# Mixture-of-experts layer of a graph network: experts as 191 register-addressed units of 196 rows instead of 64 fixed blocks of 784, 12 more tiles of edge counts beside them, and the source tiles of the clears and fills moved into the scatter stage's memory

## The chip, the cores and the metric

One Trainium2 chip, one core. The metric is the device time of one execution in microseconds (us), lower is better. The engines are PE (TensorE, matrix products), DVE (VectorE), ACT (ScalarE), POOL (GpSimd) and SP (SyncE, which here only issues DMA transfers and loads its registers). Each engine runs its own list of instructions in order and waits on semaphores. DMA transfers are issued from SP's list, from ACT's (both plain copies) and from POOL's (indirect gathers and scatters of rows).

## The reference

Four graph layers on 12,500 nodes of 128 features with 200,000 edges (`src` random, `dst` sorted and skewed towards low numbers). After each layer `x = layernorm(x + layer(x))`.

- Layer 0: points on a hyperbolic ball, a weighted sum over each node's edges, and the way back.
- Layer 1: a normalised sum over the edges times `W_conv` (`new_feats`), then a mixture of experts, then batch normalisation over the nodes of the sum of both.
- Layers 2 and 3: two more edge sums, the last followed by a small network and a residual.

The experts are what the change touches:

```
scores = x @ gate_W + gate_b                    # 12,500 x 64
topv, topi = top_k(scores, 2)                   # each node goes to two experts
pos = rank of the pair (node, expert) within its expert;  valid = pos < 782
buf[expert, pos] = x                            # 64 x 782 x 128, zero where no pair is
y = gelu(buf @ W1 + b1) @ W2 + b2               # W1 128x256, W2 256x128 per expert
out = sum over the two experts of softmax(topv) * y[expert, pos]
```

25,000 pairs go into 64 experts of at most 782 rows, so about half of the rows of `buf` are blank.

## The kernel before, in words

The nodes are 98 tiles of 128 (`NT`, `P`). The stages follow each other, and the end of each is marked by what the next reads; times are those of the profiled execution.

**Preparation (0 to about 200 us).** `points` (lines 446 to 487) maps the nodes to the ball and writes 14 groups of rows (`table<-parts`); columns of the edge list are loaded and turned (lines 531 to 630). On SP's list among these stand clears of `msg` (`clear`, line 523, the source is the tile `blank`, 396 KB each, 99 in all and three smaller ones for the last tile) and fills of `buf` with zeros (line 670, the source is the tile `zero`, 448 KB each, 56 in all). `msg` is a DRAM array in which every edge will have a row, and a row without an edge must hold zeros; `buf` holds the experts' rows. Tile, the framework that the kernel is written in, puts the instructions of most stages into an order of its own, so SP's list doesn't follow the text: 51 of the clears and 8 of the fills are issued in this stage.

**Scatter (213 to 2734 us).** `spread_edges` (lines 489 to 770) runs 391 iterations of 512 edges. In each, `fetch` (lines 654 to 670) broadcasts the edges' row numbers (`rb`), loads a number from `first_r` into an SP register (line 657), and loads the window of table rows at that address (`win`, line 661); every so often it also issues a clear or, in every sixth iteration, a fill. PE picks the edges' rows by one-hot products (lines 695 and 701), DVE multiplies them by the weights (line 722), ACT casts them into one of six `rows` buffers (line 734), and POOL scatters them into `msg` (line 751). The order of DVE, PE and ACT is written out by hand here (`manual_schedule`); SP's and POOL's is the scheduler's.

**Collecting, first edge sums, routing (2740 to 5124 us).** Collecting reads `msg` back in large transfers. The routing (lines 1314 to 1393) forms `new_feats` and the gate scores, takes the top two, and counts per expert in the tile `run` (each partition its part of the pairs per expert), from which each pair's row `expert * SL + pos` follows. POOL scatters 196 times 128 rows into `buf` (line 1388), the last one starting at 5122.1 us. `SL` is 784 rows per expert, seven tiles of `TT` = 112.

**Experts (5124 to 5716 us, lines 1398 to 1442).** For each of 64 experts: SP loads `w1` and `w2` (lines 1411, 1413; 128 KB each), ACT's list loads a broadcast bias `b2` and the 784 rows `xt` (lines 1415, 1417), PE transposes seven tiles (line 1422), DVE copies them into `bT` (lines 1423, 1424), four products of 392 columns (line 1429) go to PSUM, ACT does the gelu (line 1431), fourteen products (line 1436) give `pw` again, DVE adds the bias (line 1439) and SP stores 784 rows to `ybuf` (line 1440). All addresses are fixed.

Beside the experts stand the **band counts** (`band_counts`, line 1252) of the later edge sums: for a node tile, DVE makes one-hot marks (`fs` line 1073, `fd` line 1075), PE multiplies them in about 17 matmuls (`fb_ps`, line 1089), ACT casts four banks (line 1091) and SP stores 512 KB (line 1093). `EXB` = 48 of the 98 tiles are written in the experts' loop, the other 50 in the combining loop; the scheduler interleaves them with their neighbours, and starts some before the first expert.

**Combining (5716 to 6045 us, lines 1470 to 1480).** For each node tile POOL gathers 128 rows of `ybuf` twice (`yk`, line 1476), DVE multiplies by the gates and adds (line 1479), `stats` accumulates the sums of the batch normalisation (line 1451). Then the normalisation and the two last edge sums, up to 8278 us.

Of the kernel before, what the change touches and what calls it, by code (L numbers as in the profile page):

```python
# [40 lines left out]
TT = 112  # L41
NTT = 7
SL = TT * NTT
# [24 lines left out]
EXB = 48  # L68
# [70 lines left out]
def gnn_kernel(ctx: ExitStack, tc: tile.TileContext, a, out: bass.AP):  # L139
# [65 lines left out]
    ybuf = dram.tile([DUMP, D], F32, name="ybuf")  # L205
# [283 lines left out]
    def spread_edges(bad):  # L489
# [5 lines left out]
        with tc.tile_pool(name="sc", bufs=1) as pc, tc.tile_pool(name="scp", bufs=1, space=PSUM) as pps:  # L495
# [19 lines left out]

            blank = pc.tile([P, RB - SURE, W3], BF16, name="blank")
            V.memset(blank, 0.0)
            V.memset(blank[:, :, 3 * W0:3 * W0 + 1], -1.0)
            V.memset(blank[:, :, 3 * W0 + 1:3 * W0 + 3], 127.0)

            def clear(t, b0, b1):
                r0 = t * RS
                return Y.dma_start(msg[r0 + b0 * P:r0 + b1 * P, :].rearrange("(b p) f -> p b f", p=P),
                                   blank[:, 0:b1 - b0, :])

            if True:
# [105 lines left out]
                px_.close()  # L632
                for b in range(SURE_LAST, RB, RB - SURE):
                    clear(NT - 1, b, min(b + RB - SURE, RB))

            with tc.tile_pool(name="sb", bufs=4) as lp, tc.tile_pool(name="sw", bufs=3) as wk, \
                    tc.tile_pool(name="sg", bufs=2, space=PSUM) as gp:
                step = 7 * D
                zero = pc.tile([P, step], F32, name="zero")
                V.memset(zero, 0.0)  # L640
                bz = buf[0:DUMP, :].rearrange("(p r) f -> p (r f)", p=P)
                empty = list(range(NT - 1))
                fill = list(range(0, DUMP // P * D, step))
# [10 lines left out]
                def fetch(i):  # L654
# [13 lines left out]
                    if i % 6 == 5 and fill:  # L668
                        r = fill.pop(0)
                        Y.dma_start(bz[:, r:r + step], zero)  # L670
# [631 lines left out]
    with tc.tile_pool(name="moe", bufs=1) as pm:  # L1302
# [95 lines left out]
        with tc.tile_pool(name="ex", bufs=2) as wk, tc.tile_pool(name="exb", bufs=2, space=PSUM) as pb, \  # L1398
                tc.tile_pool(name="exh", bufs=2, space=PSUM) as ph_, tc.tile_pool(name="exc", bufs=1) as pc, \
                band_pools("x") as band:  # L1400
            b1n = pc.tile([NE, HID], F32, name="b1n")
            Y.dma_start(b1n, a["L1_gnn_b1"])
            b1T = pc.tile([P, 2, NE], F32, name="b1T")
            for j in range(2):
                pb1 = ph_.tile([P, 512], F32, name="ph")
                T.transpose(pb1[:, 0:NE], b1n[:, j * P:(j + 1) * P], ident[:NE, :NE])
                V.tensor_copy(b1T[:, j, :], pb1[:, 0:NE])
            HALF = SL // 2
            for e in range(NE):
                w1 = wk.tile([P, HID], F32, name="w1")  # L1410
                Y.dma_start(w1, a["L1_gnn_W1"][e])
                w2 = wk.tile([P, 2, D], F32, name="w2")
                Y.dma_start(w2, a["L1_gnn_W2"][e].rearrange("(j p) d -> p j d", p=P))
                b2 = wk.tile([TT, D], F32, name="b2")
                S.dma_start(b2, a["L1_gnn_b2"][e].partition_broadcast(TT))
                xt = wk.tile([TT, NTT, D], F32, name="xt")
                S.dma_start(xt, buf[e * SL:(e + 1) * SL, :].rearrange("(i p) f -> p i f", p=TT))
                px = pb.tile([P, 1024], F32, name="pw")
                bT = wk.tile([P, SL], F32, name="bT")
                for i in range(NTT):  # L1420
                    o = i * TT if i < 4 else 512 + (i - 4) * TT
                    T.transpose(px[:, o:o + TT], xt[:, i, :], ident[:TT, :TT])
                V.tensor_copy(bT[:, 0:4 * TT], px[:, 0:4 * TT])
                V.tensor_copy(bT[:, 4 * TT:SL], px[:, 512:512 + 3 * TT])
                hT = wk.tile([P, 2, SL], F32, name="hT")
                for j in range(2):
                    for q in range(2):
                        ph = ph_.tile([P, 512], F32, name="ph")
                        T.matmul(ph[:, 0:HALF], w1[:, j * P:(j + 1) * P], bT[:, q * HALF:(q + 1) * HALF],
                                 start=True, stop=True)  # L1430
                        S.activation(hT[:, j, q * HALF:(q + 1) * HALF], ph[:, 0:HALF], AF.Gelu,
                                     bias=b1T[:, j, e:e + 1])
                py = pb.tile([P, 8, D], F32, name="pw")
                for i in range(NTT):
                    for j in range(2):
                        T.matmul(py[:TT, i, :], hT[:, j, i * TT:(i + 1) * TT], w2[:, j, :],
                                 start=(j == 0), stop=(j == 1))
                ye = wk.tile([TT, NTT, D], F32, name="ye")
                V.tensor_tensor(ye, py[:TT, 0:NTT, :], b2[:, None, :].to_broadcast([TT, NTT, D]), OP.add)
                Y.dma_start(ybuf[e * SL:(e + 1) * SL, :].rearrange("(i p) f -> p i f", p=TT), ye)  # L1440
                for s in range(EXB * e // NE, EXB * (e + 1) // NE):
                    band_counts(band, s)
# [168 lines left out]
```

## Time and profile before

| | us |
|---|---|
| median of six executions | 8261.73 |
| lowest, highest | 8241.03, 8314.44 |
| the profiled execution: its time | 8280.44 |
| the profiled execution: its span in the trace | 8278.6 |
| preparation | 0 to about 200 |
| scatter | 213 to 2734 |
| experts, from the first weight load to the end | 5124.5 to 5716 |
| combining | 5716 to 6045 |

PE is busy 63% of the span, DVE 52%, POOL 47%, ACT 24%; the mean granted clock of PE is 0.919. Shares over the whole span say little here, because each stage has its own limit; they are read stage by stage.

How to read the lines: a group's line has the line of the kernel, the engine, the operation, `out<-in` by the program's names, the shapes where asked for, a count, then busy time in us, mean duration of one in ns, and the engine's idle time just before these instructions with what ended it. An engine's name with q (SPq, ACTq) is its list of issued transfers and register operations; their durations are given as minimum/median/maximum in ns.

### The profile page before, as it was taken

How to read it: one execution, taken by the hardware profiler on the slowest of the kernel's cores; microseconds unless marked ns; L12 is line 12 of the kernel's file. 1: busy time of each engine (PE TensorE's matmuls, PEld its weight loads, DVE VectorE, ACT ScalarE, POOL GpSimd, SP SyncE). 2: the span in 40 equal slices, each digit the busy share in tenths (PEclk: the TensorE clock that was granted, in tenths of full speed). 3: DMA queues.
4: the chain of work that ended last, by engine and by line, in shares of the span. 5: the costliest groups of instructions: out<-in, count | busy, mean ns of one | idle time of the engine just before them, and what ended most of it. 6: DMA issues, size and time to landing. Idle time of an engine off the chain costs nothing. (4 is left out here: it accounts for less than half of the span.)

```text
span 8278.6 us, 106434 instructions
## 1 busy us (share of the span) xinstructions
PE 5230.9 (63%) x32620; PEld 3153.9 (38%) x33009; DVE 4299.5 (52%) x11730; ACT 1976.7 (24%) x4176; POOL 3863.5 (47%) x3917
## 2 busy tenths in 40 slices
PE   0444444444444556388878644998717988588995
PEld 0333333333333223144444423765303444234444
DVE  6666666666666678655555355555881123301115
ACT  3222222232222122222222111443440001100003
POOL 0555555566666100366665454002716665466650
PEclk9999999999999988699999856998958999799998
DMA  9865444444444899444444312554346778577762
GB/s 225 205 168 155 139 120 120 120 122 121 122 120 121 267 324 323 129 136 132 135 133 128 96 35 72 165 166 132 129 146 204 252 244 268 159 229 250 243 231 63
DMA packets 1046137, 1375.96 MB, mean 166 GB/s; under 512 B 106732, under 2 KB 848744, under 8 KB 1045566
## 3 DMA queue, kind: packets, MB, share of 16 engines
q1 hardware_dynamic: 803208, 960.67, 39.5%
q0 software_dynamic: 181312, 376.38, 14.8%
q10 hardware_dynamic: 61046, 31.77, 1.4%
q8 instruction: 301, 4.93, 0.3%
q14 instruction: 270, 2.21, 0.1%
HBM read 911.40 MB, written 457.00 MB: 165 GB/s over the span
## 5 line engine op out<-in xcount | busy, mean ns | idle before, releaser
L1134 POOL DMA_INDIRECT fg<-table,e_row x1952 | 1932.8, 990 | 2069.5 <-SPq L1023 672.3
L1125 PE MATMUL dense<-fc_a,fc_x 128*128 128x512 bf16 x7422 | 1942.6, 387 | 344.3 <-DMA fc_x<-table 211.3
L751 POOL DMA_INDIRECT msg<-rows,to x1564 | 1501.6, 960 | 1218.9 <-DVE g_ps L722 551.1
L701 PE MATMUL g_ps<-rows,minus 128*128 128x258 bf16 x1564 | 462.7, 399 | 1165.3 <-ACT rows L734 953.1
L734 ACT CAST rows<-g_ps 128x516 bf16<-128x516 f32 x1173 | 698.6, 596 | 1790.6 <-remote 1066.1
L1089 PE MATMUL fb_ps<-fd,fs 128*128 128x512 bf16 (+7 forms) x3942 | 895.3, 349 | 349.9 <-ACT fc_a L1091 145.0
L1227 DVE TENSOR_TENSOR AT<-AT,fps 128x512 f32 x122 | 84.0, 688 | 1977.5 <-PE fps L1151 948.2
L1125 PEld LDWEIGHTS <-fc_x 128*128 128x128 bf16 x7644 | 684.1, 99 | 986.2 <-issue 371.5
L695 PE MATMUL g_ps<-win,hot 128*128 128x129 bf16 x4692 | 650.8, 311 | 272.8 <-DMA win<-table 127.2
L1075 DVE TENSOR_SCALAR fd<-iota_h,hd 128x128 bf16<-128x128 f16 (+6 forms) x1563 | 793.3, 509 | 0.0
L722 DVE TENSOR_TENSOR g_ps<-g_ps,w_c 128x516 f32<-128x516 f32 x391 | 295.7, 756 | 901.4 <-PE g_ps L707 880.6
L1151 PEld LDWEIGHTS <-fg 128*128 128x128 bf16 x5856 | 469.4, 100 | 590.5 <-issue 198.8
L701 PEld LDWEIGHTS <-minus 128*128 128x128 bf16 x1564 | 199.7, 128 | 1293.2 <-issue 1293.0
L695 PEld LDWEIGHTS <-hot 128*128 128x128 bf16 x4692 | 535.9, 143 | 350.7 <-issue 264.4
L1151 PE MATMUL fps<-fh,fg 128*128 128x96 bf16 x5856 | 586.5, 211 | 103.3 <-issue 81.6
L1089 PEld LDWEIGHTS <-fs 128*128 128x128 bf16 x4108 | 389.0, 100 | 663.7 <-issue 414.0
L1091 ACT CAST fc_a<-fb_ps 128x512 bf16<-128x512 f32 x588 | 344.1, 585 | 918.5 <-PE fb_ps L1089 457.4
L1476 POOL DMA_INDIRECT yk<-ybuf,come x196 | 230.5, 1176 | 673.7 <-DMA counts<-bc_a 593.1
L868 PE MATMUL ce_sum<-ce_r,ce_s 128*128 128x390 bf16 x1764 | 375.8, 379 | 257.9 <-DVE ce_s L865 250.2
L679 DVE TENSOR_TENSOR_SCAN run_ps<-one_ps,run_ps,bin 99x512 f32<-99x512 f32 x390 | 505.5, 1296 | 13.8
L1073 DVE TENSOR_SCALAR fs<-iota_b,hs 128x128 bf16<-128x128 bf16 x1563 | 413.3, 266 | 134.3 <-PE fb_ps L1089 103.5
L868 PEld LDWEIGHTS <-ce_s 128*128 128x128 bf16 x1764 | 188.2, 111 | 445.6 <-DVE ce_s L865 263.2
(382 smaller groups left out, 6188.8 us busy)
## 6 DMA issues: line engine op xcount, KB each, us to landing
ce_r<-msg SPq DMA_DIRECT2D x98, 1782.0 KB
fc_a<-counts SPq DMA_DIRECT2D x196, 768.0 KB
fc_a<-counts SPq DMA_DIRECT2D x196, 512.0 KB
rb<-rows_d SPq DMA_DIRECT2D x391, 256.0 KB
counts<-fc_a SPq DMA_DIRECT2D x98, 768.0 KB
counts<-bc_a SPq DMA_DIRECT2D x98, 512.0 KB
fc_x<-table SPq DMA_DIRECT2D x490, 96.0 KB
msg<-blank SPq DMA_DIRECT2D x99, 396.0 KB
```

The costliest lines, as they stand in the source:

```text
L679: V.tensor_tensor_scan(c, one_ps, b, st["end"], OP.mult, OP.add)
L695: T.matmul(gps[i][:, q, 0:D + 1], hot[i][:, q * P:(q + 1) * P], win[i][:, k, :], start=(q == 2 * half and k == 0), stop=False)
L701: T.matmul(gps[i][:, 2 * h:2 * h + 2, 0:D + 1], minus, r[:, 2 * h:2 * h + 2, k * W0:k * W0 + D + 1], start=False, stop=True, skip_group_ch ...
L734: S.copy(r[:, :, k * W0:k * W0 + D + 1], gt)
L751: sc = G.indirect_dma_start(out=msg[:, :], out_offset=bass.IndirectOffsetOnAxis(ap=to[:, q:q + 1], axis=0), in_=r[:, q, :], in_offset=None)
L868: T.matmul(ps, sel[:, j, :], r[:, j, 0:3 * W0], start=(j == 0), stop=(j == RB - 1))
L1073: V.tensor_scalar(sel, iota_b, hs[:, s, j:j + 1], None, op0=OP.is_equal)
L1075: V.tensor_scalar(col[:, 0:hi - lo], iota_h[:, 0:hi - lo], hd[self.i][:, s, q:q + 1], None, op0=OP.is_equal)
L1089: T.matmul(ps[:, lo - c0:hi - c0], self.sel[s, j], self.col[s, j][:, lo - w[j][0]:hi - w[j][0]], start=(j == first), stop=(j == js[-1]))
L1125: T.matmul(dense[n], xr[s][:, k, :], cnt[s][:, n * BANK:(n + 1) * BANK], start=(s == 0 and k == 0), stop=(s == NT - 1 and k == 2))
L1134: G.indirect_dma_start(out=g[q][:, i].rearrange("p k f -> p (k f)"), out_offset=None, in_=table[:, :], in_offset=bass.IndirectOffsetOnAxis ...
L1151: T.matmul(ps[:, ds(at[0], LW)], g[i // 4][:, i % 4, k, :], hot[i // 4][:, i % 4, :], start=False, stop=(i == WC - 1 and k == 2))
```

## The change

1. `TT` becomes 98, and a unit is `UR` = 196 rows. An expert's 784 rows are four units (`UE`). If an expert has n pairs, only its first ceil(n/196) units are worked on. At most `NU` = 191 units can be needed, and the loop runs 191 times whatever the data are; surplus iterations work on a spare place behind `ybuf`, which grows by 191 units.
2. A table of the units is made on the chip after the routing: from `run`, summed over partitions by PE, some 22 small DVE operations give for each unit its expert, the expert's bias offset, its input unit and its output unit; PE transposes the table, and it goes by DMA to DRAM (`unit_d`) and back into one partition (`unit_r`).
3. Each iteration loads numbers from `unit_r` into registers: SP two (the expert, for `w1` and `w2`; the output unit, for the store), ACT two (the input unit, for `xt`; the expert, for the gelu's bias), DVE one (the bias offset). Weights are loaded once per unit, not once per expert.
4. The second bias is no longer loaded per expert. All of it is broadcast to 98 partitions once, ahead of the loop (`b2r`).
5. The loop's SBUF pool has three buffers instead of two; PSUM has two buffers each of `px`, `ph` and `py`.
6. Since units without pairs are not computed, the rows of `ybuf` that they would fill must not hold leftovers: `ybuf` is filled with zeros as `buf` is. There are 112 fills instead of 56, in every third iteration of the scatter loop instead of every sixth.
7. `blank` and `zero` move to a new pool, `late`, that is opened after the preparation's memory is released. The clears of the last tile move behind it too.
8. `EXB` goes from 48 to 60.

The order of SP's list in the built program, which follows from 6 and 7: preparation has no clear and no fill; clears stand in the scatter loop's first 80 iterations (25, 27, 28 and 20 per 20 iterations), fills in its first 150 (8, 9, 9, 15, 30, 16, 17 and 8 per 20).

The core of the diff:

```diff
-TT = 112
-NTT = 7
-SL = TT * NTT
+TT = 98
+UR = 2 * TT
+UE = 4
+SL = UR * UE
+NU = (N * TOPK + NE * (UR - 1)) // UR
-EXB = 48
+EXB = 60
-    ybuf = dram.tile([DUMP, D], F32, name="ybuf")
+    ybuf = dram.tile([DUMP + NU * UR, D], F32, name="ybuf")
+    unit_d = dram.tile([8, P], I32, name="unit_d")
...
-            blank = pc.tile([P, RB - SURE, W3], BF16, name="blank")
...
+            with tc.tile_pool(name="late", bufs=1) as lt, tc.tile_pool(name="sb", bufs=4) as lp, tc.tile_pool(name="sw", bufs=3) as wk, \
+                    tc.tile_pool(name="sg", bufs=2, space=PSUM) as gp:
+                step = 7 * D
+                zero = lt.tile([P, step], F32, name="zero")
+                V.memset(zero, 0.0)
+                blank = lt.tile([P, RB - SURE, W3], BF16, name="blank")
...
-                fill = list(range(0, DUMP // P * D, step))
+                blanks = [b[0:DUMP, :].rearrange("(p r) f -> p (r f)", p=P) for b in (buf, ybuf)]
+                fill = [b[:, r:r + step] for b in blanks for r in range(0, DUMP // P * D, step)]
...
-                    if i % 6 == 5 and fill:
-                        r = fill.pop(0)
-                        Y.dma_start(bz[:, r:r + step], zero)
+                    if i % 3 == 2 and fill:
+                        Y.dma_start(fill.pop(0), zero)
...
+            b2r = pc.tile([TT, NE * D], F32, name="b2r")
+            Y.dma_start(b2r, a["L1_gnn_b2"].rearrange("e d -> (e d)").partition_broadcast(TT))
             b1n = pc.tile([NE, HID], F32, name="b1n")
             Y.dma_start(b1n, a["L1_gnn_b1"])
...
+                t_ps = pb.tile([P, 2, UR], F32, name="ph")
+                T.matmul(t_ps[:, 0, 0:NE], ones, run, start=True, stop=True)
+                n = pu.tile([P, NE], F32, name="un_n")
+                V.tensor_scalar_min(n, t_ps[:, 0, 0:NE], float(CAP))
...
+                Y.dma_start(unit_d, w_i)
+                Y.dma_start(unit_r, unit_d.rearrange("w p -> (w p)").rearrange("(o c) -> o c", o=1))
...
+            for j in range(NU):
+                e = number(0, j, ET.SP, NE - 1)
+                w1 = wk.tile([P, 1, HID], F32, name="w1")
+                Y.dma_start(w1, w1s[:, ds(e, 1), :])
+                w2 = wk.tile([P, 1, 2, D], F32, name="w2")
+                Y.dma_start(w2, w2s[:, ds(e, 1), :, :])
+                xt = wk.tile([TT, 1, 2, D], F32, name="xt")
+                S.dma_start(xt, rows_in[:, ds(number(2, j, ET.Activation, NE * UE - 1), 1), :, :])
+                px = pb.tile([P, UR], F32, name="px")
+                for i in range(2):
+                    T.transpose(px[:, i * TT:(i + 1) * TT], xt[:, 0, i, :], ident[:TT, :TT])
+                bT = wk.tile([P, UR], F32, name="bT")
+                V.tensor_copy(bT, px)
+                ph = pb.tile([P, 2, UR], F32, name="ph")
+                hT = wk.tile([P, 2, UR], F32, name="hT")
+                e1 = number(0, j, ET.Activation, NE - 1)
+                for k in range(2):
+                    T.matmul(ph[:, k, :], w1[:, 0, k * P:(k + 1) * P], bT, start=True, stop=True)
+                    S.activation(hT[:, k, :], ph[:, k, :], AF.Gelu, bias=b1T[:, k, ds(e1, 1)])
+                py = pb.tile([P, 2, D], F32, name="py")
+                for i in range(2):
+                    for k in range(2):
+                        T.matmul(py[:TT, i, :], hT[:, k, i * TT:(i + 1) * TT], w2[:, 0, k, :],
+                                 start=(k == 0), stop=(k == 1))
+                ye = wk.tile([TT, 1, 2, D], F32, name="ye")
+                e2 = number(1, j, ET.DVE, (NE - 1) * D)
+                for i in range(2):
+                    V.tensor_tensor(ye[:, 0, i, :], py[:TT, i, :], b2r[:, ds(e2, D)], OP.add)
+                st = Y.dma_start(rows_out[:, ds(number(3, j, ET.SP, NE * UE + NU - 1), 1), :, :], ye)
+                if j:
+                    tc.declare_no_dep(st.ins, group="units", reason="each unit has rows of its own")
+                tc.add_to_no_dep_group("units", st.ins)
+                for s in range(EXB * j // NU, EXB * (j + 1) // NU):
+                    band_counts(band, s)
```

`number(kind, j, engine, most)` loads entry j of the table's row `kind` into a register of one engine.

## The prediction

> **What bounds the kernel now.** I began with the slices of the page, cut the span at the stages the change touches, and asked for the busy time of each engine there (columns: stretch, length, PE, PEld, DVE, ACT, POOL busy, clock, DMA share, GB/s).
>
> ```profile
> 0.00:195.00 195.00, 10.52 (x49) 8.45 (x49) 121.78 (x182) 58.94 (x70) 3.79 (x8) 1.00 1.04 224
> 195.00:2740.00 2545.00, 1203.05 (x9384) 939.56 (x9384) 1590.89 (x3919) 743.53 (x1568) 1501.61 (x1564) 1.00 0.50 136
> 5124.00:5716.00 592.00, 577.78 (x3449) 407.33 (x3513) 294.17 (x710) 251.01 (x438) 0.00 (x0) 0.99 0.55 163
> 5716.00:6045.00 329.00, 243.29 (x915) 101.82 (x934) 259.38 (x817) 124.11 (x220) 230.54 (x196) 0.87 0.36 116
> ```
>
> Four limits: preparation is limited by DMA (share 1.04), the scatter stage by no busy engine, the experts by PE (578 of 592), the combining of the experts' rows by no one engine, with DVE and POOL highest.
>
> Next I asked for the scatter's pace in two stretches, by line 722, which runs once per 512 edges. The first stretch still issues 46 clears of `msg` and 43 zero fills of `buf`, the second neither.
>
> ```profile
> 213.00:872.00 659.00, 75.26 (x100) 1.00 0.64 174
> 1001.00:2665.00 1664.00, 197.12 (x260) 1.00 0.45 121
> ```
>
> 659/100 = 6.59 us against 1664/260 = 6.40: the 89 transfers cost 19 us, 0.21 each.
>
> Then the expert stage's groups by shape, and a stretch of PE in order of time, where the spacing of queued matmuls (28 in 3.29 us less the last one's own 0.27) is the price, not their mean.
>
> ```profile
> L1436 PE MATMUL pw<-w,hT 128*112 128x128 f32 x1792 | 211.6, 274 | 0.0
> L1429 PE MATMUL ph<-bT,w 128*128 128x392 f32 x512 | 205.0, 518 | 0.4
> L1431 ACT ACTIVATE hT<-ph,b1T 128x392 f32<-128x392 f32 x256 | 150.5, 588 | 85.5 <-PE ph L1429 79.2
> L1439 DVE TENSOR_TENSOR ye<-pw,b 112x896 f32<-112x896 f32 x64 | 69.9, 1092 | 249.5 <-PE pw L1436 249.5
> ```
>
> ```profile
> 5300.77 3.29 PE L1436 MATMUL pw<-w,hT 128*112 128x128 f32 x28
> ...
> 5305.55 0.84 PE L1422 MATMUL pw<-ident,xt 112*128 112x112 f32 x7
> ...
> 5307.37 1.58 PE L1429 MATMUL ph<-bT,w 128*128 128x392 f32 x4
> ```
>
> So (a float32 matmul is several records) 3.04, 0.70 and 8 x 0.326 = 2.6 us: 6.34 per expert, 406 for 64. The order of the instructions puts 744 matmuls of the band counts (43.8 tiles at 3.0 us, 131 us) among them: 537 of the 585 us from the first transposes at 5131.4 to 5716. PE waits once for data, at the start: 15.1 us for `xt`.
>
> Last, what a DMA with an address from a register costs SP, at the one place that has it, the scatter's window fetch (minimum/median/maximum in ns):
>
> ```profile
> L657 SPq TENSOR_LOAD <-first_r x391: 262/282/1195, 203.6 to 2698.7; - x196
> ```
>
> ```profile
> L661 SPq DMA_DIRECT2D win<-table x391: 13/338/520, 209.3 to 2701.4; - x196
> ```
>
> ```profile
> 209.33 2.92 SPq L661 DMA_DIRECT2D win<-table  x4
> ```
>
> Four load-and-fetch pairs in 2.92 us: (2.92 - 0.34)/3 = 0.86 us a pair. From 213 to 500 us, with the DMA engines busy, the median load is 0.501.
>
> **Part by part, against the profiled execution** (8280.4 us; its span is 8278.6, and it is 18.7 above the median of the six runs, 8261.7).
>
> A. Preparation. Before, SP sends 51 clears (396 KB) and 8 fills (448 KB) into this DMA-bound stage, each taking 1.7 to 2 us of the issue list (six clears 10.37 and 11.72 us). Now their source tiles take memory that preparation used, so all wait for its end. The table's 14 groups come every 6.5 us from 110.5; two buffers and a landing of 4.9 us allow about 5.8, so 10 us goes. The row "ACT parts waits for DMA table<-parts", 32.4 us in ten waits, is the ceiling. What is late next is VectorE's own 122 us of the 195. I take **-20** (-10 to -30).
>
> B. Scatter. The 59 transfers come here, and filling `ybuf` adds 56: 115 more than before, at 0.21 us: **+24**. All stand on SP's list ahead of window fetches. Low end +8: they share cover that the existing ones use, since this loop waits mostly for a buffer behind POOL's scatter (1066 us of ACT's idle time at line 734), no engine. High end +50: they come denser, 33 to 37 per 20 iterations over the first 80 instead of 26 to 28 at most, and one at twice the price is no surprise.
>
> C. Start of the experts. Both versions' first SP transfer waits for the last scatter into `buf`, until 5124.5. Then, before, weights and `xt`: first transposes 5131.4. Now: all biases on 98 partitions, 3.2 MB, at the 300 GB/s that the collecting stage reaches, 11 us; `b1n` behind it lands at about 5137; the table's 22 small VectorE operations with two PE steps, about 11 us among band marks; two DMAs in series (out and back) 5 to 6; a load and fetch with its landing 3 to 4; PE's in-order neighbours some 4. First transposes near 5162: **+31** (25 to 40). Five more band tiles are done meanwhile (8 rather than 3.2 ahead of the first expert), counted in D and E.
>
> D. Units. 64 experts of 784 rows are 50,176 rows; 191 units of 196 are 37,436. PE per unit: 2 transposes 0.2, 2 products of 196 columns 0.65, 4 back 0.87: 1.72, so 328 us, with 52 band tiles 156: **484**. This is no longer the only tight queue. SP per unit has two loads, four register-addressed transfers (two weight loads share a register), 0.27 counts stores: 2 x 0.86 + 0.52 + 0.09 = 2.33 us, 445 in all; with the loaded 0.501 and the maximum of 0.520 per transfer, 2 x (0.50 + 0.07 + 0.52) + 0.52 + 0.13 = 2.83, **541**. ACT gets two gelus of about 0.4 (between 0.588 at 392 columns and the half), 1.1 casts of 0.6, two loads and a transfer: 1.5 busy plus up to 1.2 of issue, 2.7 at worst (516). VectorE stays near 2. PE's 484 at the present ratio (585/537) is 527. Three queues at 2.5 to 2.8 us a unit, tied by two or three buffers and fixed orders, do not run at the slowest one's pace: I take 2.93 us, **560 us, -25**. Bounds: 484 (PE alone) and 649 (3.4 us, rival 2). Unit 191 costs what unit 1 costs: the loop always runs all of them, though 25,000 pairs can fill as few as 128; so there the change does less than its words say.
>
> The DMA engines are no limit by the rows: they are busy 55% of 592 us, 326 us for 96.6 MB; the new stage moves 119 MB (three times the weights, fewer rows), 401 us.
>
> A page of the Trainium skill speaks against the new tile height: "DMA: Bandwidth & Descriptors", section "Why a DMA increments its semaphore by 16 and not by 1", says that a transfer uses the largest number of engines up to 16 that divides its slowest dimension: 16 for 112 partitions, 14 for 98. No row here shows a 98-partition transfer; by the rule, as an estimate, the row transfers (a third of the bytes) would crowd on 14 engines and the busiest would have 419 us instead of 401, and the sum is the same.
>
> E. Combining. 50.8 band tiles are left after the experts before, 37.9 now: 13 fewer. POOL's gathers (196 x 1.18 = 231 us, 245 with their spacing) are the floor under this stage; DVE spends some 3.7 us a tile. Fully on the path that is -48; if only the visible waits go,
>
> ```profile
> POOL yk L1476 <- DVE ACC L1479: 25.7, 15, 8.0
> ...
> POOL yk L1476 <- DVE fs L1073: 18.3, 60, 0.3
> ```
>
> half of their 44 us, -18. I take **-33**.
>
> Sum: -20 + 24 + 31 - 25 - 33 = -23: 8257 in the profile's frame, **8239** in that of the median.
>
> **Rivals.**
> 1. PE alone paces the units: loop 484 (-101), combining -45: -20 + 24 + 31 - 101 - 45 = -111, **8151**. For it: before, PE waits for nothing else. Against: SP had 4 transfers per 9 us expert, now 4 per 2.9 us.
> 2. Slower: SP's queue paces. The place is its list in the unit loop, where each weight load waits for the buffer that PE just released and the store for VectorE; if two such hand-overs of 0.3 us a unit are not covered, 2.83 becomes 3.4: 649, +64, in sum +66, **8328**. It decides from 3.27 us a unit (624 us): there the total is 0.5% above before.
> 3. The gain is given back: units at 3.06 us (585, nothing won), scatter at its +50: -20 + 50 + 31 + 0 - 33 = +28, **8290**. For it: ACT at 2.7 and SP at 2.8 us leave PE little to win.
>
> **How the numbers follow.** About 0.5% (41 us) is what a measurement of this kernel can tell from no change. Forecast 0.42 (its own range 8200 to 8280), rival 1 0.18, rival 2 0.18, rival 3 0.22. Faster takes rival 1 and a third of the forecast: 0.34. Slower takes rival 2 and a third of rival 3: 0.25. The rest, 0.41, is the same. The range 8145 to 8335 leaves out about half of rivals 1 and 2.
>
> **What would show it.** A: line 722's first instance some 20 us earlier. B: its pace over the first 150 iterations, 6.55 or 6.7 us. C: first transposes 31 us later than before's, net of A and B. D: the distance of successive unit stores, 2.5, 2.9 or 3.4 us, and whose wait stands before PE: its own band tiles (rival 1), DMA for weights with SP never idle (rival 2). E: the stretch from the last unit to the normalisation, 33 us shorter. A gain outside these stages, or edge sums that move by over 10 us, would make the accounting wrong.

## The result and the profile after

The changed kernel takes 8357.0 us (median of 20 executions, 8320.7 to 8384.4), the kernel before 8279.5 (median of 46, 8241.0 to 8318.1). The ratio is 1.0094, with a 95% interval of 1.008 to 1.0108: 0.9% slower, 78 us. The forecast was 8239, and the range ended at 8335; on the scale of the forecast's 8261.7 the measured ratio gives 8339, just outside.

Where the time went, from the same marks in both traces (us; the marks are the first and last instructions of the groups named):

| stretch | before | after | difference | forecast |
|---|---|---|---|---|
| to the first weighting of the scatter (line 722, after 724) | 213.3 | 192.6 | -21 | -20 |
| its first 150 iterations | 983.3 | 1002.7 | +19 | +24 |
| its other 241 | 1531.3 | 1516.7 | -15 | 0 |
| collecting | 710.9 | 712.8 | +2 | 0 |
| first edge sums | 1337.0 | 1355.5 | +19 | 0 |
| routing | 346.3 | 340.8 | -6 | 0 |
| last scatter into `buf` to the first transposes | 9.3 | 36.1 | +27 | +31 |
| first transposes to the last bias add | 580.4 | 651.8 | **+71** | **-25** |
| combining (to POOL's last gather) | 315.5 | 301.4 | -14 | -33 with the next |
| normalisation | 178.8 | 163.6 | -15 | |
| last two edge sums | 2072.5 | 2063.0 | -10 | 0 |
| span | 8278.6 | 8337.0 | +58 | -23 |

The stages of the changed kernel's profile, columns as before:

```profile
0.00:195.00 195.00, 13.67 (x81) 11.29 (x82) 132.15 (x203) 63.68 (x76) 3.80 (x8) 0.71 0.49 127
...
5157.00:5810.00 653.00, 569.51 (x3501) 421.59 (x3558) 358.03 (x1189) 274.09 (x593) 0.00 (x0) 0.99 0.59 179
5810.00:6111.00 301.00, 201.32 (x705) 83.23 (x720) 214.63 (x665) 95.56 (x169) 225.97 (x196) 0.84 0.33 106
```

Preparation's DMA share fell from 1.04 to 0.49. In the experts PE, which was busy 578 of 592 us, now is 570 of 653: there is 83 us in which nothing runs on it. The scatter's pace, by line 724 in two stretches of the same kernel:

```profile
192.00:851.00 659.00, 73.74 (x98) 0.50 0.84 223
980.00:2644.00 1664.00, 200.37 (x262) 0.50 0.47 128
```

659/98 = 6.72 us an iteration with the transfers against 1664/262 = 6.35 without. Groups of the experts by shape:

```profile
L1489 PE MATMUL py<-w,hT 128*98 128x128 f32 x1528 | 238.5, 279 | 9.0 <-ACT hT L1485 4.2 <-DMA w<-in_L_gnn_W 2.6 <-DVE ye L1494 0.4
L1484 PE MATMUL ph<-bT,w 128*128 128x196 f32 x764 | 213.2, 361 | 60.5 <-ACT hT L1485 34.9 <-DMA w<-in_L_gnn_W 21.3 <-DVE bT L1479 0.9
L1485 ACT ACTIVATE hT<-ph,b1T 128x196 f32<-128x196 f32 x382 | 162.3, 425 | 307.3 <-PE ph L1484 156.6 <-DMA xt<-buf 58.4 <-PE fb_ps L1091 46.8
L1494 DVE TENSOR_TENSOR ye<-py,b2r 98x128 f32<-98x128 f32 x382 | 93.5, 286 | 148.4 <-PE py L1489 134.4 <-DMA ybuf<-ye 4.5 <-DMA xt<-buf 3.6
```

Before, the product into `ph` had 0.4 us of idle time in front of it; now it has 60.5, half behind the gelu of ACT and a third behind the weights of SP. ACT's gelu in turn stands 58.4 us behind the issue of `xt` on its own list. The operations on the lists:

```profile
L1458 SPq TENSOR_LOAD <-unit_r x379: 262/458/1193, 5157.3 to 5806.2; - x190
```

```profile
L1458 ACTq TENSOR_LOAD <-unit_r x379: 272/451/1387, 5157.5 to 5803.1; - x190
```

```profile
L1474 ACTq DMA_DIRECT2D xt<-buf x189: 565/567/857, 5156.8 to 5779.4; - x189
```

In order of time, a stretch of ACT and its list, with the idle time and its end in brackets:

```profile
5407.31 0.57 ACTq L1474 DMA_DIRECT2D xt<-buf  x1
5408.01 0.43 ACT L1485 ACTIVATE hT<-ph,b1T 128x196 f32<-128x196 f32 x1 [0.93 <-DMA xt<-buf]
5409.29 0.42 ACT L1485 ACTIVATE hT<-ph,b1T 128x196 f32<-128x196 f32 x1 [0.85 <-PE ph L1484]
```

The first gelu stands behind the issue of `xt`, and a register load of 1.05 us on the same list lies between the two gelus. A register load has a median of 0.45 us and at times 1.2 to 1.4, on both lists; a transfer with an address from a register occupies ACT's list for 0.57 us, where the fixed one before took 0.33. The Trainium skill, "DMA: Bandwidth & Descriptors", section "Latency and other measured facts", gives a register load a floor of about 600 ns; here the shortest take 262 and half are under 460, so the measurement decides.

### The profile page after: what moved, and what is told of

Its sections match the earlier page's. It is cut to its first block, busy times and chain, and to the rows that moved or that the text cites. A ratio compares the mean times of both kernels' runs of the same rounds, so it can differ in the third digit from the quotient of the medians.

```text
span 8337.0 us, 111407 instructions
## 1 busy us (share of the span) xinstructions
PE 5217.5 (63%) x32555; PEld 3164.4 (38%) x32934; DVE 4341.7 (52%) x12135; ACT 1987.4 (24%) x4302; POOL 3878.0 (47%) x3918
## 5 line engine op out<-in xcount | busy, mean ns | idle before, releaser
L1091 PE MATMUL fb_ps<-fd,fs 128*128 128x512 bf16 (+7 forms) x3951 | 925.0, 351 | 365.9 <-ACT fc_a L1093 150.9
L1091 PEld LDWEIGHTS <-fs 128*128 128x128 bf16 x4108 | 391.6, 100 | 651.8 <-issue 430.4
L1534 POOL DMA_INDIRECT yk<-ybuf,come x196 | 226.0, 1153 | 762.4 <-DVE fs L1075 702.2
```

Source lines behind the costliest of these rows:

```text
L1091: T.matmul(ps[:, lo - c0:hi - c0], self.sel[s, j], self.col[s, j][:, lo - w[j][0]:hi - w[j][0]], start=(j == first), stop=(j == js[-1]))
```

## The experiments

The kernels ran in five groups, each group on one chip together with the kernel before, which took 7063, 8120, 8268, 7063 and 8284 us there (the third and the fifth group had the same chip). Nearly half of the difference comes from the scatter, which runs at 5.1 us an iteration on the chips of the first and fourth group and at 6.2 to 6.35 on the others, the rest mostly from the edge sums and the routing. So times are compared by the ratio to the kernel before in the same group. The experts' loop doesn't share this: the changed kernel's took 651.8, 651.8 and 649.4 us in three profiles, that of before 580.4, 579.9 and (in a kernel with the same loop) 579.4.

The theories: **S**, SP's list paces the units (the prediction's rival 2); **A**, register loads and the issue of `xt` stand ahead of the gelus on ACT's list; **G**, it is the grain, five hand-overs a unit; and later **P**, PE had no slack before, and a band tile costs it some 3.2 to 3.7 us.

**Addresses fixed: all, ACT's, SP's.** These three compute something else, as their expectations say.

```diff
+                fe = min(j // 3, NE - 1)
-                e = number(0, j, ET.SP, NE - 1)                  # e1_all_fixed, e3_sp_fixed; the store likewise
+                e = fe
-                e1 = number(0, j, ET.Activation, NE - 1)         # e1_all_fixed, e2_act_fixed; xt likewise
+                e1 = fe
-                e2 = number(1, j, ET.DVE, (NE - 1) * D)          # e1_all_fixed alone
+                e2 = fe * D
```

> The changed kernel with the register loads of the unit loop taken out on SP, ACT and DVE: unit j has the fixed expert j//3 and fixed rows, so the output isn't the reference's, but the number and size of transfers, products, gelus and adds stay. The unit loop (first transposes to last add) took 652 us. Theory S (SP's list paces) and theory A (loads and the issue of xt stand ahead of the gelus on ACT's list): the loop falls to 530-570 us, the total by 80-120. Theory G (the grain: five hand-overs per unit between PE, DVE and ACT in a fixed order, whatever the addresses): it stays at 620 or above, the total within 30 us.

> Only ACT's register loads are taken out (rows of xt and bias of the gelu at fixed addresses; the output isn't the reference's), SP and DVE as in the changed kernel. Theory A: loop 570 us or less. Theory S: 640-655. Theory G: 620 or above. If S and A share it, about half of what the kernel without any loads gains.

> Only SP's register loads are taken out (weights loaded and rows stored at fixed addresses; the output isn't the reference's), ACT and DVE as in the changed kernel. Theory S: loop 570 us or less. Theory A: 640-655. Theory G: 620 or above.

Since transposes that don't wait for the table start earlier, start and loop are taken together (from the last scatter into `buf` to the last bias add; before 589 us, changed 688):

| kernel | ratio to before (95%) | start and loop, us |
|---|---|---|
| all fixed | 1.0044 (1.0030 to 1.0057) | 583 |
| ACT's fixed | 1.0162 (1.0145 to 1.0179) | 670 |
| SP's fixed | 1.0259 (1.0242 to 1.0276) | 738 |

Without any load it falls by 105 us, some 30 of them the table's start: theory G as the whole cause is out. But neither S nor A alone passes: freeing ACT gave 17 us, freeing SP cost 50, where each theory had expected a loop of 570 us or less. PE's busy time in the loop with all fixed:

```profile
4297.00:4874.00 577.00, 556.68 (x3633) 424.91 (x3634) 368.33 (x1255) 277.75 (x607) 0.00 (x0) 0.98 0.69 211
```

PE is busy 557 of 577 us: even without register loads on any list this loop, with its 12 tiles more, is no faster than that of before (580), because PE itself is nearly full. That was not in the prediction, which gave PE 484. With SP fixed PE hardly waits for weights any more (21.3 us in the changed kernel), but it waits longer for gelus, and the reason stands on ACT's list:

```profile
PE ph L1486 <- ACT hT L1487: 97.0, 58, 2.8
...
PE ph L1486 <- DMA w<-in_L_gnn_W: 0.4, 1, 0.4
```

```profile
ACT hT L1487 <- DMA xt<-buf: 156.1, 98, 3.8
```

The scheduler wrote another order for it. On PE's list a unit's transposes stand on average 1.6 units ahead of its first product, where they stand 4.1 ahead in the changed kernel; an issue of `xt` stands 4.0 units ahead of the gelus beside it instead of 6.8; and a gelu waits behind an `xt` whose buffer isn't free. So this kernel doesn't isolate SP, but it shows where ACT's list hurts. The kernel with all addresses fixed has a short order too (1.7 units), so its gain isn't free of the order either.

**The load of `xt` on POOL's list**, which is empty in this stage.

```diff
-                S.dma_start(xt, rows_in[:, ds(number(2, j, ET.Activation, NE * UE - 1), 1), :, :])
+                G.dma_start(xt, rows_in[:, ds(number(2, j, ET.Pool, NE * UE - 1), 1), :, :])
```

> The load of xt goes from ACT's list to POOL's, which has nothing to do in this stage; ACT keeps one register load per unit. Computes the same. Theory A: loop 590 us or less, total some 60 us less than the changed kernel. Theory S and G: loop within 15 us of 652; a slower issue on POOL would show as PE waiting for xt.

Ratio 1.0159 (1.0141 to 1.0177); start and loop 664 us, 24 less, and the loop 629. PE's waits in it:

```profile
PE ph L1484 <- DMA w<-in_L_gnn_W: 25.0, 32, 2.2
PE ph L1484 <- ACT hT L1485: 7.2, 20, 0.6
```

PE's wait for the gelu fell from 35 to 7 us; the wait for SP's weights stayed (21 in the changed kernel, 25 now). Between the 590 and the 637 of the two expectations: A is part of it.

**Only the clears and fills moved; only EXB 60; only 140 units.** The first two are made from the kernel before.

```diff
 # f4_before_late: spread_edges as in the changed kernel, all else as before
 # f5_before_exb60
-EXB = 48
+EXB = 60
 # g1_140_units, from the changed kernel
-NU = (N * TOPK + NE * (UR - 1)) // UR
+NU = 140
```

> The changed kernel again, beside the kernel before and the three other kernels of this call, as their reference: unit loop near 650 us, ratio to the kernel before 1.01 on a chip on which it takes 8280 us; where the scatter runs faster and the whole is 7063, the same 80 us more would be 1.011 to 1.015.

> Before with the scatter part of the change alone: blank and zero tiles in the later pool, 112 fills in every third iteration (parts A and B), experts and combining as before. By the prediction -20 in preparation and +24 in the scatter's first 150 iterations: total within 10 us of before. If the later fills also disturb what follows (the first edge sums took 18 us longer in the changed kernel's profile), 15 to 25 slower, with the first edge sums longer here too; if that was the clock, they are as long as in the other kernels of this call.

> Before with EXB 60 instead of 48, nothing else: 12 band tiles go from the combining stage to the experts. Theory P (PE has no slack in the expert stage of before; a band tile is 3.7 us of PE): experts +40 to 45, combining and normalisation -30, total +5 to +20. Had PE the slack that the prediction gave it (48 us of 585): experts +10 or less, total -20 or more.

> The changed kernel with 140 units instead of 191: as many as this input's pairs fill, so it is right for this input but not for every one. Theory P with the register loads' cost on top (3.4 us a unit): unit loop 190 - 10 less the time of the band tiles that stay, 52 tiles in fewer units: 480 to 520 us instead of 652, total 130 to 170 less than the changed kernel and about 60 to 90 less than before. If the band tiles or the DMA paced the loop, less than 80 comes off.

| kernel | ratio (95%) | to first weighting | 150 iterations | first edge sums | start and loop | combining, normalisation |
|---|---|---|---|---|---|---|
| changed | 1.0109 (1.0075 to 1.0143) | 186.7 | 954.7 | 1334.3 | 687.6 | 459.6 |
| clears and fills alone | 1.0002 (0.9976 to 1.0028) | 187.1 | 956.0 | 1308.8 | 589.0 | 462.2 |
| EXB 60 alone | 1.0049 (1.0028 to 1.0069) | 203.8 | 941.8 | 1343.2 | 628.7 | 466.7 |
| 140 units | 1.0045 (1.0023 to 1.0068) | 188.7 | 961.9 | 1327.4 | 617.9 | 459.9 |

The moved clears and fills give 17 us in preparation and take 14 in the scatter: nothing, as forecast. The first edge sums vary by 34 us between these profiles without any order by part (the kernel with the moved fills has the shortest), so the +19 of the first pair is no effect of them. The -15 of the other 241 iterations is no more than profiles on one chip differ by (1526 to 1540 us in the third and fifth group).

EXB 60 alone makes the loop of before 39.7 us longer, 3.3 us a tile, and gives nothing in combining that can be told from the others (466.7 against 462.2 with EXB 48). So the total rose by 40 us, not by the 5 to 20 expected: the 30 us expected back from combining didn't come. For the loop, theory P is confirmed by its profile:

```profile
5035.00:5654.00 619.00, 618.75 (x3714) 424.27 (x3713) 337.92 (x850) 277.46 (x482) 0.00 (x0) 1.00 0.56 163
```

PE is busy 618.75 of 619 us.

140 units took 70 us off the loop: 1.4 us for each unit left out, less than a unit's own work. Theory P with the loads' cost on top had expected a loop of 480 to 520 us and was wrong here (582); under 80 us off was the expectation if the band tiles or the DMA engines set the pace. The waits name neither, but ACT's list. The scheduler's order is a short one here too (transposes 1.8 units ahead of their product), so the 70 us aren't the price of the surplus units alone. The loop's waits for the gelu and, from ACT's side, behind `xt`:

```profile
PE ph L1484 <- ACT hT L1485: 78.6, 60, 2.5
```

```profile
ACT hT L1485 <- DMA xt<-buf: 86.1, 49, 3.7
```

**`xt` on POOL with 140 units; `xt` and `w2` on POOL; EXB 48; a branch for the surplus units.**

```diff
 # h1_xt_w2_pool, from the kernel with xt on POOL
-                Y.dma_start(w2, w2s[:, ds(e, 1), :, :])
+                G.dma_start(w2, w2s[:, ds(number(0, j, ET.Pool, NE - 1), 1), :, :])
 # h2_140_xt_pool: xt on POOL, NU = 140        # f3_after_exb48: EXB = 48
 # h3_branch: h1, EXB = 48, and
+                V.tensor_scalar(mf, end[0:1, NE - 1:NE], 140.0, None, op0=OP.is_gt)
+                V.tensor_copy(more_i, mf)
...
+        more = nc.values_load(more_i[0:1, 0:1], min_val=0, max_val=1)
+        with tc.If(more > 0):
+            for j in range(140, NU): unit(j, wk, pb)
```

> The changed kernel with xt and w2 loaded from POOL's list (one register load and one transfer each there), so that ACT's list has no transfer of the loop and SP's has one weight load less. Computes the same. Moving xt alone took 24 us off start and loop (688 to 664). Theory A+S (transfers and loads ahead of other work on ACT's and SP's lists make PE wait): start and loop 620 or less, that is the 583 of all addresses fixed plus the table's 30. If PE then still waits for weights, it is the loads' own latency and the result stays near 660.

> 140 units (enough for this input only) and xt loaded from POOL's list. With 140 units alone the loop took 582 us though PE's own work is near 470, PE waited 79 us for gelus, and ACT's gap lay behind the issue of xt. Theory A: loop 500 to 520, total 60 to 80 less than with 140 units alone. If the order of PE's list around the band tiles is what costs: 560 or more.

> The changed kernel with EXB 48. Theory P (a band tile is 3.2 to 3.7 us wherever PE is short, and nothing in the combining stage, whose end POOL's gathers set): loop 652 - 40 = 612, combining within 5 us of the changed kernel's 298, total 35 to 45 less than the changed kernel, within 0.6% of before. By the prediction's terms it would be slower than the changed kernel: +33 in combining for a loop that is not bound by PE.

> For every input: 140 units always, the other 51 in a branch that is taken only if the table has more than 140; xt and w2 from POOL's list; EXB 48. Sum of the three effects: 140 units with xt on POOL 510, 12 band tiles less 40: loop about 470, start 36, branch 5, combining 300: start and loop 510 against 589 of before, total 65 to 85 less than before (ratio 0.99). If the branch costs 30 us or more, or POOL's two transfers a unit are late, the gain is under 40.

| kernel | ratio (95%) | start and loop | combining, normalisation |
|---|---|---|---|
| `xt`, `w2` on POOL | 1.0121 (1.0100 to 1.0142) | 711 | 481 |
| 140 units, `xt` on POOL | 0.9913 (0.9895 to 0.9930) | 513 | 482 |
| EXB 48 | 1.0116 (1.0077 to 1.0154) | 664 | 482 |
| branch, `xt`, `w2` on POOL, EXB 48 | 0.9977 (0.9958 to 0.9996) | 561 | 480 |

140 units with `xt` on POOL: the loop fell from 582 to 475 us, further than the 500 to 520 expected, and PE is busy in nearly all of it:

```profile
5158.00:5633.00 475.00, 451.67 (x2785) 325.74 (x2836) 310.58 (x1036) 228.75 (x487) 105.09 (x138) 1.00 0.64 194
```

```profile
PE ph L1484 <- ACT hT L1485: 2.1, 6, 0.6
```

The wait for the gelu went from 78.6 to 2.1 us: there theory A is shown. `w2` on POOL as well was a miss of mine (711 us, 620 or less expected): POOL's list is in order too, and its `w2` waits for a buffer with the next unit's `xt` behind it.

```profile
PE px L1477 <- DMA xt<-buf: 91.7, 99, 3.6
```

The transposes, which had waited 3 us for `xt` with `xt` alone on POOL, now wait 92. The same held the branch kernel at 561, where 510 was expected. EXB 48 took 24 us off the loop, not 40, and nothing off the total, where 35 to 45 were expected: the ratio is 1.0116, and that of the changed kernel on this chip 1.0080 (below); combining and normalisation took 482 us against its 468.

**What a kernel for every input keeps.** On another chip, with the kernel before beside them:

```diff
 # j1_branch_xt_pool: branch, xt on POOL, w2 on SP, EXB = 60      # j2_branch_exb48: EXB = 48
 # j4_table_first, from j1: the table's block ahead of the biases, and
-            Y.dma_start(b2r, a["L1_gnn_b2"].rearrange("e d -> (e d)").partition_broadcast(TT))
+            G.dma_start(b2r, a["L1_gnn_b2"].rearrange("e d -> (e d)").partition_broadcast(TT))
-            Y.dma_start(b1n, a["L1_gnn_b1"])
+            S.dma_start(b1n, a["L1_gnn_b1"])
```

> The kernel before, profiled on the same chip as the three others of this call, as reference for the stages after the experts. The combining stage and the normalisation took 316 and 179 us in its first profile, 298 and 164 in one of its relatives with the same instructions there, so that the changed kernel's 301 and 164 may be no gain: if the change's gain there is real (theory of the prediction, 33 us), this profile has 25 to 40 us more in the two stages than the kernels with EXB 60 beside it; if it was the execution, within 10.

> For every input: 140 units always, the other 51 in a branch taken only where the table has more; xt loaded from POOL's list, both weights from SP's, EXB 60. With 140 units fixed and xt on POOL start and loop took 513 us. The branch should cost what a jump and a register load cost, under 10 us: start and loop 520, total 60 to 75 less than before (ratio 0.992). With w2 on POOL as well it was 561, because PE waited for xt behind w2 on POOL's list; if that was not the reason, this one is near 560 too.

> As the kernel with the branch and xt on POOL, with EXB 48. Where band tiles cost PE 3.7 us in the loop and fit into the combining stage for less: loop 35 to 45 less, combining and normalisation 5 to 20 more, total 20 to 35 less. Where the combining stage is as full as the prediction had it (2.5 us a tile): total within 10.

> As the kernel with the branch, xt on POOL and EXB 60, with the table of the units made first and the two biases loaded beside it (b1 from ACT's list, b2 from POOL's), instead of 3.2 MB ahead of the table on SP's list. Start 36 us before; the transfer of the biases is about 12 of them: start 22 to 26, total 10 to 14 less than without it. If the table's chain, not the transfer, holds the start, under 4.

| kernel | ratio (95%) | to first weighting | 150 iterations | start | loop | combining, normalisation |
|---|---|---|---|---|---|---|
| before | one execution, 7068 us | 210.3 | 749.0 | 9.4 | 579.9 | 449.1 |
| branch, `xt` on POOL | 0.9956 (0.9944 to 0.9969) | 190.2 | 816.8 | 36.0 | 479.3 | 450.1 |
| the same, EXB 48 | 0.9945 (0.9929 to 0.9962) | 190.5 | 795.3 | 35.4 | 469.5 | 448.6 |
| EXB 60, table first | 0.9932 (0.9916 to 0.9949) | 190.9 | 801.8 | 25.5 | 473.6 | 452.4 |

The branch, which this input doesn't take, costs nothing that shows: start and loop 515 against 513. EXB 48 took 10 us off this loop, not the 35 to 45 expected: PE's busy time fell by 21 us (456 to 435), its wait for weights ahead of `ph` rose from 12.5 to 18.7, and the lists' order is another one again. The 12 band tiles gain nothing in combining (449.1, 450.1 and 448.6, with 50, 38 and 50 left there). The table ahead of the biases saves 10.5 us of the start, which with 25.5 us is within the 22 to 26 expected; what is left over the 9.4 of before is the table's own chain. The total gain was smaller than expected by what the scatter lost: +46 to +68 us in the first 150 iterations, against +14 and +19 on the slower chips. Line 722 (after: 724) over those iterations, in the kernel before and in the one with `xt` on POOL, which has all of the change's fills, two chips of the same pace:

```profile
210.00:960.00 750.00, 107.24 (x151) 1.00 0.78 206
```

```profile
190.00:991.00 801.00, 107.00 (x150) 1.00 0.95 254
```

Where an iteration takes 5 us, the DMA engines are already busy 0.78 of this stretch, and the added transfers nearly fill them (0.95); where it takes 6.5 there was room (0.84 with them, by the stretch shown with the result). That this is why the price differs is argued from these shares; no run tested it.

**All remedies together, and the change beside it.** `m1_both` is the kernel with the table first, with EXB 48.

> For every input, the three edits that helped, together: 140 units always and the rest in a branch, xt on POOL's list, the table first with the biases beside it, EXB 48. Start and loop 490 against 589 of before, combining as before, preparation and scatter together within 35 us of before: total 60 to 75 less where before takes 7063, 85 to 105 less where it takes 8120 to 8280 (ratio 0.988 to 0.991).

> The changed kernel on the same chip as the one with the three edits: 1.010 to 1.015 of before; start and loop 688 us again whatever the chip's scatter pace is, since the loop took 652 us on two chips.

The three edits together: ratio 0.9878 (0.9855 to 0.9901), 8186 us against 8284, start and loop 496 (start 25.0, loop 470.5). The changed kernel on the same chip: 1.0080 (1.0053 to 1.0107), 686. So 191 us of start and loop separate them, and 174 us of the total (for the changed kernel 1.010 or more was expected). PE in the new loop:

```profile
5141.00:5612.00 471.00, 435.11 (x2647) 311.54 (x2691) 282.04 (x928) 215.26 (x454) 100.04 (x137) 0.99 0.61 186
```

```profile
PE ph L1491 <- DMA w<-in_L_gnn_W: 19.5, 27, 2.2
PE ph L1491 <- ACT hT L1492: 4.3, 14, 0.6
```

PE is busy 435 of 471 us. Of what is left, SP's weights are the largest wait, and the gelu is 4 us. This version is the best of the study and faster than both kernels. It is written for every input, though no run had one that takes the branch.

## Why the prediction was wrong, point by point

**A and B, preparation and scatter, right** on chips like that of the forecast: -21 and +19 in the first pair, -17 and +14 in the part made alone, its total 1.0002. The price per transfer was not a constant of the kernel: 0.12 to 0.17 us on those chips, 0.4 to 0.6 (46 to 68 us over 115 transfers) where the scatter runs faster.

**C, the start, right:** +27 for +31; in every kernel whose loop waits for the table behind the biases the start is 35 to 38 us, against 9, and the biases' 11 us measured 10.5 when they were moved. The DMA engines, at a mean share of 0.59 in the new loop, gave no sign of being a limit, so that the number of engines that a 98-partition transfer uses had no occasion to show.

**D failed, at the step "Three queues at 2.5 to 2.8 us a unit, tied by two or three buffers and fixed orders, do not run at the slowest one's pace: I take 2.93 us".** This left 0.10 us a unit, 19 us in all, above the slowest queue (541) for what the queues cost each other. It measured about 100: the loop took 652 us, and PE's own work in it comes to some 551 (worked out below). Most of it comes from register-addressed work on in-order lists: with all addresses fixed the loop is 577, 75 us less, in an order of its own. PE's listed waits in the changed loop sum to 77, most of them the two named above, 34.9 behind the gelu and 21.3 behind SP's weights. No list was full: SP's was occupied 472 of 653 us and ACT's, with its engine, 455. Each holds PE up in turn, because a gelu stands behind the issue of `xt` or a register load, as the stretch of ACT shows, and a weight load behind SP's own loads (PE's wait for weights went from 21.3 to 0.4 us with SP fixed). The pace of 3.41 us a unit is the number of rival 2, 3.4, but not its mechanism, so that its 8328 came near is luck.

PE's own price was too low as well, 484 for 551. By itself this would not have missed, since 551 is 9 us under the 560 taken; against the 580 of before it is about the gain that D forecast, and the 100 us turn it into +71. The first view that the prediction shows has PE busy 577.78 of 592 us, and the working priced its work at 537; it carried the difference along as a ratio (527) but kept 484 as its bound. There was no slack in before's loop. Three sizes were wrong:

- An expert's matmuls cost PE 6.68 us, not 6.34 (start-to-start times in before's loop), 427 for 64. The line of four products that the prediction shows has three spacings in 1.58 less the 0.52 of one, 0.35 each, where the working has 0.326.
- A band tile costs PE 3.3 us (39.7/12), and from PE's start-to-start times in before's loop, 153 us for 43.8 tiles, 3.5. The working had 3.0. 427 and 153 are the 580 of that loop. EXB 60 put 8 more tiles into the loop, some 26 to 29 us, priced at 25.
- A unit costs PE 1.93 us, not 1.72 (start-to-start times with all addresses fixed, that loop's waits among them: `ph` 0.81, `py` 0.93, `px` 0.19; 1.89 without the waits). 191 x 1.93 is 369; with 52 tiles at 3.5, 182, the floor is 551. The same prices give 452 for 140 units, and PE was busy 451.67 us in the loop of 140 units with `xt` on POOL. Rival 1's 484 was out of reach by this sum.

**The remark on surplus units was right and had no price.** 51 of 191 units compute nothing that is used. With `xt` on POOL they cost 151 us (664 to 513 us of start and loop), 3.0 a unit, the change of the lists' order among them; with `xt` on ACT's list 70, and the kernel with 140 units alone was still slower than before (1.0045). Neither edit alone changes the sign; the two together do (0.9913).

**E, combining, failed:** forecast -33, and the first pair seemed to agree (-29). On the chip where before takes 7063, profiles with 50 and with 38 tiles left are within 4 us, and on the one with 8120 within 7; where it takes 8280, EXB 60 gives 465, 468, 481 and 482, EXB 48 gives 494, 482, 480 and 494. So it is 0 to -15, with a spread of that size. The waits that the working halved did fall in the first pair, from 44 to 27 us, but the end didn't follow them on the other chips. POOL's gathers, 230.5 us of busy time before and 226.0 after, may set it; no run showed that. A slip of the sum is small beside this: half of 44 is 22, not 18. Another is in the chances: rival 1 and a third of the forecast make 0.32, not 0.34.

**Open:** with 191 units and `xt` on POOL the loop is 629 us, some 80 above PE's sum. PE's listed waits there are some 45 us; the rest is a wider spacing of PE's own matmuls (2.03 us a unit, 3.7 a band tile), and no run took it apart. How the cost divides between ACT's and SP's lists is open too: no kernel freed SP's list with the order of the others unchanged. DVE's load was taken out only together with the others; PE's waits behind DVE in the changed loop are 2 us. Nor is it shown why 12 tiles fewer gave 24 and 10 us where PE's price says 40.

## What to carry to other kernels

When an engine is busy 98% of a stage and a sum of priced instructions gives 92%, as here, doubt the sum before the engine: calibrate the prices until they give the busy time. When several in-order lists serve one busy engine, the slowest list's sum is no forecast: here the lists cost 100 us more than the engine's own work, and none was full. A transfer whose address is in a register costs its list a load, an issue and, worst, its place in line: put it on a list with nothing urgent behind it, and only one kind on it. Units for the worst case pay for the worst case on every input; a branch around the rarely needed ones, not taken, cost nothing that showed.

## What was not expected of the hardware

The recorded granted clock differs with no difference in time: in the 150 iterations of the scatter it is 1.00 before and 0.50 after (the stretches of the scatter shown with the prediction and with the result), with the same spacing of consecutive matmuls of one line (108 ns, median, for line 695, after 697), and executions of the changed kernel with a mean clock of 0.75 and of 0.915 have medians of 8341 and 8359 us.

The chips differ in one stage above all: POOL's scatter instruction takes 960 ns (median) on both, yet an iteration takes 6.35 us on one and 5.06 on another. Over the same 900 us of the scatter, ACT's largest wait ahead of its work on a `rows` buffer (line 726 copies three columns into it, line 734 casts the rest) is, in the kernel before on the first chip and on the other:

```profile
ACT rows L734 <- remote: 376.9, 69, 6.6
```

```profile
ACT rows L726 <- DMA msg<-rows,to: 264.5, 175, 2.6
```

Spread over the iterations, that is 2.7 us for each of 142 and 1.5 for each of 178. The second profile names the scatter's DMA, the first no cause; why the chips differ in it no run told.
